# The last FFN's first batch: rows turned by VectorE's blocks and DMA instead of TensorE's transposes

## The chip, the cores and the metric

The kernel runs on one core of a Trainium2 chip. A core has five engines that run their own instruction streams and wait for one another by semaphores: TensorE (PE, matrix products; its weight loads are listed as PEld), VectorE (DVE), ScalarE (ACT), GpSimd (POOL) and SyncE (SP, which here only issues DMAs). The metric is the device time of one execution in microseconds, lower is better; a version's time is the median of its runs.

## The reference

Two transformer layers with post-layernorm, all float32, on `x` of 8 batches x 512 tokens x 512 features. The change lies where layer 1's attention meets layer 1's FFN:

```python
x = L0_attn_x
x = _layernorm(x + _L0_attn_ref(x, ...))    # 16 heads, causal
x = _layernorm(x + _L0_ffn_ref(x, ...))     # 8 experts, the two best per token, LoRA merged
x = _layernorm(x + _L1_attn_ref(x, ...))    # 8 query heads, 2 key/value heads of 64, no mask; adds its own input once more
x = _layernorm(x + _L1_ffn_ref(x, ...))

def _L1_ffn_ref(x, wq_gate, s_gate, wq_up, s_up, wq_down, s_down):
    def _qlinear(x, wq, scale):             # integer weights, hidden width 1408
        W = (wq.astype(jnp.float32) - 128.0) * scale[:, None]
        return jnp.einsum('bsd,hd->bsh', x, W)
    gate = jax.nn.silu(_qlinear(x, wq_gate, s_gate))
    up = _qlinear(x, wq_up, s_up)
    return _qlinear(gate * up, wq_down, s_down)
```

## The kernel before

A batch is 512 tokens: NT = 4 tiles of 128 tokens, and ND = 4 chunks of 128 features. `xs[b]` holds a batch with tokens on the partitions. A matrix product over the features needs them on the partitions, so each batch's rows must be turned before it enters a layer.

**Two ways to turn.** TensorE can transpose 128x128 blocks against an identity into PSUM. The class `Turn` does it without TensorE: `Turn.blocks` has VectorE transpose each token tile in blocks of 32x32 (line 88, one instruction for a tile, four for a batch); `Turn.out` writes the result to DRAM in four DMAs (line 93), and `Turn.back` reads it back in one (line 96), with the blocks at their places. The four writes wait for all four block transposes, the read waits for the four writes. The tokens of such a turned batch lie in another order within a chunk; `Turn.by_tile` gives a view of an array in that order, and whoever leaves the turned layout applies it once.

**Layer 1's attention** (`Attention1.batches`, line 1644). For each batch, 4 groups of query heads (`g`) times 4 key tiles (`kt`) make 16 units, handled in 8 *slots* of two units each. A slot does, in this order:

- `score` of its two units: on PE the scores, on ACT the exponential (line 1705) into `p`, a tile of four buffers, so that unit u takes the buffer of unit u - 4;
- `add` of the two units of the slot before: DVE sums the probabilities of a group into `total` (line 1713); the first key tile of a group is not added alone but together with the second;
- the slot's extra pieces, `todo[i]`;
- `product` of the two units of the slot before (PE, line 1724);
- where these closed a group, `normalise`: PE sums `total` over the keys (`rs`, line 1732), ACT reads the sums (line 995), DVE takes the reciprocal (line 1735) and multiplies (line 1742), GpSimd adds to a guard.

The extra pieces come from `plan(b)`: output projections of the batch before (`project`: PE line 1670, then DVE's residual line 1676 and statistics lines 1684 and 1685), the queries of groups 1 to 3 (`query`: PE line 1607, ACT's copy line 1609), and what prepares the next batch, among it that batch's rows turned by `Turn`. These read `hT`, the batch's turned rows: one buffer in the pool `c_own`. The last batch (`final`, b = 7) has no next batch to prepare. It has instead, in slots 0, 2, 4 and 6, the four pieces of `IntegerFfn.split` for the FFN's first batch, b = 0, whose rows have long been through their layernorm.

On PE, DVE, ACT and POOL the order of the instructions in this stage is the order of the program (`in_order`): an instruction that waits holds back all that stand behind it on its engine. SP's queue is placed by the framework. PSUM tiles named by `mm` rotate through two banks.

After the last slot the code adds and multiplies the last two units, projects token tile 0 over the first three groups, closes the last group with `normalise`, projects the rest, adds the residuals and takes the statistics; then the FFN begins.

**The last FFN** (`IntegerFfn`). Its products run in a faster format (F32R) on two halves of each value, so a batch's turned rows come as `high` (a cast) and `low` (the rest). For batch 0 `split` makes them: sixteen transposes on PE (line 1108, four for each chunk), ACT's cast out of PSUM (line 1109), DVE's subtraction (line 1110). For the later batches `blocks` and `parts` do it within the FFN: `Turn`, then the cast (line 1098) and the subtraction (line 1099) from SBUF. `hidden` makes the hidden layer (PE line 1143, ACT and DVE lines 1146 to 1154) and splits it again, for b > 0 through `by_tile` so that the tokens come back to their order:

```python
hT, *halves = [self.turns[0].by_tile(a, back) if b else a for a, back in ((hT, True), (high, False), (low, False))]
```

Of the kernel before, what the change touches and what calls it, by code (L numbers as in the profile page):

```python
# [9 lines left out]
F32 = mybir.dt.float32  # L10
# [4 lines left out]
ALU = mybir.AluOpType  # L15
# [3 lines left out]
P = 128  # L19
NB = 8  # L20
S = 512
D = 512
NT = S // P
ND = D // P
# [48 lines left out]
class Turn:  # L73
# [11 lines left out]
    def blocks(self, room, t, x):  # L85

        out = room.rearrange("p (j t c) -> p j t c", t=self.n, c=32)[:, :, t, :]
        self.nc.vector.transpose(out, x.rearrange("p (j c) -> p j c", c=32))
# [977 lines left out]
class IntegerFfn:  # L1066
# [13 lines left out]
        self.halves[b] = [pool.tile([P, ND, S], F32R, tag=f"rows{i}", name=f"x3_{part}")  # L1080
                          for i, part in enumerate(("high", "low"))]

    def blocks(self, b, t):

        if t == 0:
            self.room(b)
            self.turned = self.raw.tile([P, ND * S], F32, tag="turned", name="turned")
        turn = self.turns[b % 2]
        turn.blocks(self.turned, t, self.env.xs[b][:, t, :])
        if t == NT - 1:  # L1090
            turn.out(self.turned)
            turn.back(self.turned)

    def parts(self, b, c):
# [2 lines left out]
        x = self.turned[:, ts(c, S)]  # L1097
        self.nc.scalar.copy(high, x)
        self.nc.vector.tensor_tensor(low, x, high.bitcast(F32), ALU.subtract)

    def split(self, b, c, ps):

        nc = self.nc
        if c == 0:
            self.room(b)
        high, low = self.halves[b]
        for t in range(NT):
            nc.tensor.transpose(ps[:, ts(t, P)], self.env.xs[b][:, t, ts(c, P)], self.env.ident)
        nc.scalar.copy(high[:, c, :], ps)
        nc.vector.tensor_tensor(low[:, c, :], ps, high[:, c, :].bitcast(F32), ALU.subtract)  # L1110

    def run(self, held_out, last_norm):
        tc, nc, weights = self.env.tc, self.nc, self.weights
        with ExitStack() as phase:
            self.work = phase.enter_context(tc.tile_pool(name="d_work", bufs=1))
            self.p_gu = phase.enter_context(tc.tile_pool(name="d_gu", bufs=2, space=PSUM))
            self.p_o = phase.enter_context(tc.tile_pool(name="d_o", bufs=1, space=PSUM))
            weights.open(phase.enter_context(tc.tile_pool(name="d_weights", bufs=1)), 3 * NHID - weights.at)
            self.sd = self.work.tile([P, D], F32, name="sd")
            with tc.tile_pool(name="d_slots", bufs=1) as slots:  # L1120
                while weights.at < 3 * NHID:
                    weights.load(slots, 4, 3 * NHID)
                    weights.convert()
                nc.sync.dma_start(out=self.sd, in_=self.env.ins.s_down.partition_broadcast(P))
            with tc.tile_pool(name="d_raw", bufs=1) as self.raw:
                for b in range(NB - 1):
                    self.batch(b)
                    if b == 0:
                        last_norm()
                        ps = self.p_gu.tile([1, 1], F32, tag="g", name="ps_held")  # L1130
                        nc.scalar.dma_start(out=held_out, in_=self.guard.partitions_held(self.env.const, ps))
            self.late = phase.enter_context(tc.tile_pool(name="d_late", bufs=self.HELD))
            self.batch(NB - 1)

    def hidden(self, b, c, held):

        nc, vec, work, weights = self.nc, self.env.vec, self.work, self.weights
        g = self.p_gu.tile([P, S], F32, tag="g", name="ps_g1")
        u = self.p_gu.tile([P, S], F32, tag="u", name="ps_u1")
        for ps, w in ((g, weights(2 * c)), (u, weights(2 * c + 1))):  # L1140
            for dc in range(ND):
                for i, x in enumerate(self.halves[b]):
                    nc.tensor.matmul(ps, lhsT=w[:, ts(dc, P)], rhs=x[:, dc, :],  # L1143
                                     start=(dc, i) == (0, 0), stop=(dc, i) == (ND - 1, 1))
        sg = work.tile([P, S], F32, tag="sg", name="sg1", bufs=2)
        nc.scalar.activation(sg, g, AF.Silu, scale=vec[:, V_SG + c : V_SG + c + 1])
        hT = work.tile([P, S], F32, tag="hT", name="hT2", bufs=2)
        nc.vector.scalar_tensor_tensor(hT, u, vec[:, V_SU + c : V_SU + c + 1], sg, ALU.mult, ALU.mult)  # L1148
        high, low = (self.late.tile([P, S], F32R, tag=f"h{i}", name="h_late") if held else
                     work.tile([P, S], F32R, tag=f"h{i}", name="h_half", bufs=2) for i in range(2))  # L1150

        hT, *halves = [self.turns[0].by_tile(a, back) if b else a for a, back in ((hT, True), (high, False), (low, False))]
        nc.scalar.copy(halves[0], hT)
        nc.vector.tensor_tensor(halves[1], hT, halves[0].bitcast(F32), ALU.subtract)  # L1154
        return high, low
# [381 lines left out]
class Attention1:  # L1537
# [94 lines left out]
        for part in (self.w_qkv[:, c, :], self.w_qkv[:, ND : ND + 2, ts(c, P)]):  # L1632
            self.nc.scalar.mul(part, part, self.nss[:, c : c + 1])

    def run(self, weights, split):

        with ExitStack() as phase:
            self.work = work = phase.enter_context(self.env.tc.tile_pool(name="c_work", bufs=1, reuse_waits="tile"))
            p_sc = phase.enter_context(self.env.tc.tile_pool(name="c_sc", bufs=2, space=PSUM, reuse_waits="tile"))
            p_av = phase.enter_context(self.env.tc.tile_pool(name="c_av", bufs=2, space=PSUM, reuse_waits="tile"))  # L1640
            with in_order(self.env.tc, mybir.EngineType.DVE, mybir.EngineType.Activation, mybir.EngineType.Pool):
                return self.batches(work, p_sc, p_av, weights, split)

    def batches(self, work, p_sc, p_av, weights, split):
        env, nc, guard, state, HD = self.env, self.nc, self.guard, self.state, self.HD
        xs = env.xs
        scale = 1.0 / math.sqrt(HD)
# [97 lines left out]
        def plan(b):  # L1745


            todo = [[] for _ in range(ND * NT // 2)]
            here = pieces.pop(b)
            first, final = b == 0, b == NB - 1  # L1750
            if first:
                pieces[1] = self.prepare(1)
                todo[0] += [lambda t=t: pieces[1]["fetch"](t) for t in range(NT)]
            then = pieces.get(b + 1)
            if b:
                for t, i in enumerate((2, 3, 4, 7) if final else (2, 3, 4, 5)):
                    todo[i].append(lambda t=t: project(b - 1, t))
                if not final:
                    todo[6].append(lambda: norm(b - 1))
            for g, i in zip((1, 2, 3), (1, 3, 5) if first else (0, 1, 5) if final else (0, 1, 3)):  # L1760
                todo[i].append(lambda g=g: here["query"](g))
            if final:
                for c, i in enumerate((0, 2, 4, 6)):
                    todo[i].append(lambda c=c: split(0, c, self.mm([P, S], "ps_xT")))
            else:
                if first:

                    for t, i in ((2, 1), (3, 2)):
                        todo[i].append(lambda t=t: then["sum"](t))
                        todo[i + 2].append(lambda t=t: then["stat"](t))  # L1770
                for t, i in ((0, 1), (1, 2)) if first else ((0, 0), (1, 1), (2, 1), (3, 2)):
                    todo[i].append(lambda t=t: then["add"](t))
                if first:
                    todo[4].append(then["deviations"])

                    todo[5].insert(0, then["norm"])
                    todo[6] += [lambda c=c: then["turn"](c) for c in range(ND)]
                else:
                    todo[2].append(then["deviations"])
                    todo[3].append(then["norm"])  # L1780
                    todo[3] += [lambda t=t: then["blocks"](t) for t in range(NT)]
                todo[6].append(then["key"])
                todo[7] += [then["value"], lambda: then["query"](0)]
                if b + 2 < NB:
                    after = pieces[b + 2] = self.prepare(b + 2)
                    todo[7] += [lambda t=t: after["fetch"](t) for t in range(NT)]
            for i in (7,) if first else (1, 7) if final else (5, 7):
                todo[i] += [weights.convert, lambda: weights.load(work, 2, weights.FIRST)]
            return todo

        last = []
        for b in range(NB):
            for i, thunks in enumerate(plan(b)):
                units = [(b, u // NT, u % NT) for u in (2 * i, 2 * i + 1)]
                ps = [score(*unit) for unit in units]
# [29 lines left out]
def usual_pass(tc, ins, held_out):  # L1825
    nc = tc.nc
    with ExitStack() as ctx:
# [4 lines left out]
        with tc.tile_pool(name="a_mm", bufs=2, space=PSUM) as p_mm, ExitStack() as attn1_ctx:  # L1832
# [28 lines left out]
            weights = IntegerWeights(env, guard)  # L1861
            weights.open(ctx.enter_context(tc.tile_pool(name="c_weights", bufs=1, side="right")), weights.FIRST)
            ffn = IntegerFfn(env, guard, weights, rows, dram)
            last_norm = attention.run(weights, ffn.split)
        ffn.run(held_out, last_norm)


# [304 lines left out]
```

## Time and profile before

| | |
|---|---|
| median of 3 runs | 2221.11 us (2220.45 to 2225.37) |
| profiled execution | 2228.55 us, span 2226.8 us |
| mean granted TensorE clock | 0.993 |
| busy over the span | PE 98%, DVE 57%, ACT 28%, POOL 22% |
| sixteen transposes of `split` (line 1108), first and last start | 1648.1 and 1693.7 us |
| layer 1's last batch, from its first scores to the FFN's first product | 1643.1 to 1722.8 us |
| the FFN's batches 0, 1, 2 | 63.2, 63.0, 63.0 us |

A group's row in the profile names the line, the engine, the operation and its tiles (output <- inputs). Records of a timeline are merged: the first column is the start, the second the length of the whole run of instructions, `x4` their number, and the bracket the idle time of the engine before them and what ended it. TensorE's matrix products in float32 are recorded as two instructions each. The ends of PE's records are modelled and overlap their successors a little, so distances between starts are the better measure there. In a row of stretches stand the length, the busy time and number of instructions of PE, PEld, DVE, ACT and POOL, the granted clock, the DMA engines' share and GB/s.

### The profile page before, as it was taken

To read this page: it belongs to the slowest core of one execution; us is meant where nothing else is said; L and a number is where in the kernel's file an instruction comes from. 1 tells how busy PE (TensorE), PEld (TensorE's weight loads), DVE (VectorE), ACT (ScalarE), POOL (GpSimd) and SP (SyncE) were. 2 spreads that over 40 slices of the span, in tenths; PEclk is the share of its full clock that TensorE was granted. 3 is DMA by queue.
4 is the path that set the end of the run, shared out by engine and by line. 5 is a ranking of instruction groups with operands and counts; after the bars stand their busy time and mean duration, and the time that the engine had idled before them with its cause. 6 is when DMAs were issued, how large, how long until landed. Compare 5 with 4: busy or idle time off the path is not lost. (4 is left out here: it accounts for less than half of the span.)

```text
span 2226.8 us, 23678 instructions
## 1 busy us (share of the span) xinstructions
PE 2191.9 (98%) x9006; PEld 1116.6 (50%) x9006; DVE 1273.7 (57%) x2032; ACT 632.0 (28%) x917; POOL 487.6 (22%) x489
## 2 busy tenths in 40 slices
PE   9999999999999999999999999999999999999997
PEld 3344444444444444444443333333343778888876
DVE  3556666666666633323316887798757655555443
ACT  2332323323233232122124333223332222222222
POOL 2322423234132333122105222222211000000000
PEclk9999999999999899999999999999999999999999
DMA  8010101101022216888735212312110321111000
GB/s 297 20 57 1 57 10 48 58 1 58 5 71 94 85 57 181 227 218 214 191 114 193 80 57 86 95 55 77 45 32 13 109 78 57 57 57 57 20 20 21
DMA packets 146428, 182.20 MB, mean 82 GB/s; under 512 B 60530, under 2 KB 89202, under 8 KB 144514
## 3 DMA queue, kind: packets, MB, share of 16 engines
q1 hardware_dynamic: 135024, 144.91, 21.0%
q0 software_dynamic: 10560, 34.61, 5.5%
q8 instruction: 74, 1.21, 0.2%
q10 hardware_dynamic: 722, 1.07, 0.1%
q14 instruction: 48, 0.39, 0.1%
HBM read 117.38 MB, written 63.18 MB: 81 GB/s over the span
## 5 line engine op out<-in xcount | busy, mean ns | idle before, releaser
L903 PE MATMUL ps_gu<-experts,xrT 128*128 128x512 f32 (+1 forms) x520 | 248.8, 601 | 0.0
L1360 ACT ACTIVATE p<-sc 128x2048 f32<-128x2048 f32 (+1 forms) x96 | 152.8, 1592 | 190.0 <-PE sc L1356 183.1
L1148 DVE SCALAR_TENSOR_TENSOR hT<-ps_u,vec,sg 128x512 f32<-128x512 f32 x88 | 65.6, 745 | 195.2 <-PE ps_u L1143 195.2
L1365 POOL TENSOR_SCALAR_AFFINE_SELECT p<-p 128x512 f32<-128x512 f32 x128 | 91.6, 729 | 385.2 <-ACT p L1360 378.5
L1159 PE MATMUL ps_f<-ffn_w,h_half 128*128 128x512 f32 x672 | 170.2, 394 | 0.6 <-issue 0.4
L998 POOL TENSOR_TENSOR g_total<-g_total,r_inv 128x512 f32<-128x512 f32 x64 | 89.7, 1401 | 358.3 <-DVE r_inv L1735 283.0
L1705 ACT ACTIVATE p<-sc 128x1024 f32<-128x1024 f32 x128 | 124.0, 1021 | 105.9 <-PE sc L1702 100.8
L1735 DVE RECIPROCAL r_inv<-r_inv 128x512 f32<-128x512 f32 x32 | 107.1, 3346 | 78.8 <-ACT r_inv L995 78.8
L1388 DVE TENSOR_TENSOR p<-p 128x1536 f32<-128x1536 f32 (+2 forms) x96 | 129.4, 1348 | 39.2 <-POOL p L1365 22.2
L905 DVE TENSOR_TENSOR h<-ps_gu,h 128x256 f32<-128x256 f32 x67 | 28.4, 424 | 212.8 <-ACT h L904 212.8
L903 PEld LDWEIGHTS ps_gu<-experts,xrT 128*128 128x128 f32 x520 | 96.2, 197 | 89.7 <-issue 89.5
L1159 PEld LDWEIGHTS ps_f<-ffn_w,h_half 128*128 128x128 f32 x672 | 124.4, 188 | 33.0 <-DVE h_half L1154 5.6
L1143 PE MATMUL ps_g<-x_high,ffn_w 128*128 128x512 f32 x352 | 138.9, 395 | 0.8 <-DVE x L1676 0.8
L1143 PE MATMUL ps_g<-x_low,ffn_w 128*128 128x512 f32 x352 | 139.1, 395 | 0.0
L1143 PE MATMUL ps_u<-x_low,ffn_w 128*128 128x512 f32 x352 | 138.8, 394 | 0.0
L1143 PE MATMUL ps_u<-x_high,ffn_w 128*128 128x512 f32 x352 | 138.7, 394 | 0.0
L919 PE MATMUL ps_y<-experts,hT 128*128 128x512 f32 (+1 forms) x272 | 127.9, 593 | 0.5 <-ACT hT L913 0.5
L1702 PE MATMUL sc<-qT,kT 64*128 64x512 f32 x512 | 127.3, 615 | 1.0 <-ACT qT L1609 0.7
L1292 PE MATMUL ps_q<-experts 128*128 128x512 f32 x256 | 121.1, 615 | 4.4 <-DMA experts<-in_xT 4.4
L1724 PE MATMUL av<-p,v 128*64 128x512 f32 x512 | 123.8, 605 | 0.0
L1285 PE MATMUL ps_v<-experts 128*128 128x512 f32 x256 | 118.0, 609 | 3.3 <-DVE v L1287 3.3
L1670 PE MATMUL ps_o<-attn_out,aoT 128*128 128x512 f32 x256 | 117.9, 605 | 0.8 <-ACT r_inv L995 0.8
(262 smaller groups left out, 3438.5 us busy)
## 6 DMA issues: line engine op xcount, KB each, us to landing
results<-y SPq DMA_DIRECT2D x68, 256.0 KB, 2.3
turned<-turned SPq DMA_DIRECT2D x56, 256.0 KB, 4.1
pair<-xrT SPq DMA_DIRECT2D x25, 512.0 KB, 3.4
xrT<-pair SPq DMA_DIRECT2D x100, 128.0 KB, 4.5
x<-in_x SPq DMA_DIRECT2D x8, 1024.0 KB, 7.5
experts<-in_gate_up SPq DMA_DIRECT2D x8, 1024.0 KB, 10.8
rows<-x SPq DMA_DIRECT2D x32, 256.0 KB, 2.0
x<-rows SPq DMA_DIRECT2D x8, 1024.0 KB, 15.5
```

Of the source, the lines that this page charges most:

```text
L903: nc.tensor.matmul(ps, lhsT=xT[:, c, :], rhs=self.weights(i, c), start=c == 0, stop=c == ND - 1)
L919: self.nc.tensor.matmul(ps, lhsT=hT[:, c, :], rhs=self.weights(i, ND + c), start=c == 0, stop=c == self.NI - 1)
L1143: nc.tensor.matmul(ps, lhsT=w[:, ts(dc, P)], rhs=x[:, dc, :], start=(dc, i) == (0, 0), stop=(dc, i) == (ND - 1, 1))
L1159: self.nc.tensor.matmul(os[t], lhsT=h[:, ts(t, P)], rhs=self.weights(2 * NHID + c), start=(c, i) == (0, 0), stop=(c, i) == (NHID - 1, 1))
L1285: nc.tensor.matmul(ps, lhsT=xts[b][:, c, ts(t, P)], rhs=wv[:, c, :], start=c == 0, stop=c == ND - 1)
L1292: nc.tensor.matmul(ps, lhsT=wq[:, g, ts(c, P)], rhs=xts[b][:, c, :], start=c == 0, stop=c == ND - 1)
L1360: nc.scalar.activation(p, sc[:, :, :width], AF.Exp, scale=scale)
L1388: nc.vector.tensor_tensor(total[:, :, P * kt :], total[:, :, P * kt :], p[:, :, at : at + w], ALU.add)
L1670: nc.tensor.matmul(ps, lhsT=state[b]["aoT"][:, c, ts(t, P)], rhs=w_out[:, c, :], start=c == 0, stop=c == ND - 1)
L1702: nc.tensor.matmul(sc[:, j, :], lhsT=st["kT"][hs, ts(kt, P)], rhs=st["qT"][g][hs, :], start=True, stop=True)
L1705: nc.scalar.activation(p, sc, AF.Exp, scale=scale)
L1724: nc.tensor.matmul(st["av"][HD * j : HD * (j + 1), :], lhsT=st["v"][:, kt, HD * j : HD * (j + 1)], rhs=p[:, j, :], start=kt == 0, stop=kt ...
```

## The change

The last attention batch no longer calls `split`. It calls the FFN's own `blocks` and `parts` for batch 0, as the FFN does for its later batches:

- in slot 4, after the output projection that stands there, the four block transposes of batch 0's rows, into a new tile that takes the buffer of `hT`, followed by the four DMAs to DRAM and the one back;
- in slots 6, 6, 7 and 7, the cast and the subtraction of each chunk, from SBUF;
- so that `hT` is free in time, the last batch's query of group 3 goes from slot 5 to slot 3, where the middle batches have it;
- `hidden` applies `by_tile` to batch 0 too;
- `split` and its sixteen transposes are gone.

```diff
@@ class IntegerFfn
-    def blocks(self, b, t):
+    def blocks(self, b, t, room=None):
         if t == 0:
             self.room(b)
-            self.turned = self.raw.tile([P, ND * S], F32, tag="turned", name="turned")
+            self.turned = self.raw.tile([P, ND * S], F32, tag="turned", name="turned") if room is None else room
         turn = self.turns[b % 2]
         turn.blocks(self.turned, t, self.env.xs[b][:, t, :])
         if t == NT - 1:
...
-    def split(self, b, c, ps):
-
-        nc = self.nc
-        if c == 0:
-            self.room(b)
-        high, low = self.halves[b]
-        for t in range(NT):
-            nc.tensor.transpose(ps[:, ts(t, P)], self.env.xs[b][:, t, ts(c, P)], self.env.ident)
-        nc.scalar.copy(high[:, c, :], ps)
-        nc.vector.tensor_tensor(low[:, c, :], ps, high[:, c, :].bitcast(F32), ALU.subtract)
...
-        hT, *halves = [self.turns[0].by_tile(a, back) if b else a for a, back in ((hT, True), (high, False), (low, False))]
+        hT, *halves = [self.turns[0].by_tile(a, back) for a, back in ((hT, True), (high, False), (low, False))]
@@ class Attention1, plan(b); run and batches pass the FFN itself on in place of its split
-            for g, i in zip((1, 2, 3), (1, 3, 5) if first else (0, 1, 5) if final else (0, 1, 3)):
+            for g, i in zip((1, 2, 3), (1, 3, 5) if first else (0, 1, 3)):
                 todo[i].append(lambda g=g: here["query"](g))
             if final:
-                for c, i in enumerate((0, 2, 4, 6)):
-                    todo[i].append(lambda c=c: split(0, c, self.mm([P, S], "ps_xT")))
+
+                room = []
+                def blocks(t):
+                    if t == 0:
+                        room.append(self.own.tile([P, ND, S], F32, tag="hT", name="turned2"))
+                    ffn.blocks(0, t, room[0].rearrange("p k s -> p (k s)"))
+                todo[4] += [lambda t=t: blocks(t) for t in range(NT)]
+                for c, i in enumerate((6, 6, 7, 7)):
+                    todo[i].append(lambda c=c: ffn.parts(0, c))
```

More of the change, by code (lines that the diff above doesn't have):

```diff
@@ L1633, in scale, with run @@
             self.nc.scalar.mul(part, part, self.nss[:, c : c + 1])
-    def run(self, weights, split):
+    def run(self, weights, ffn):
         with ExitStack() as phase:
@@ L1641, in run, with batches @@
             with in_order(self.env.tc, mybir.EngineType.DVE, mybir.EngineType.Activation, mybir.EngineType.Pool):
-                return self.batches(work, p_sc, p_av, weights, split)
-    def batches(self, work, p_sc, p_av, weights, split):
+                return self.batches(work, p_sc, p_av, weights, ffn)
+    def batches(self, work, p_sc, p_av, weights, ffn):
         env, nc, guard, state, HD = self.env, self.nc, self.guard, self.state, self.HD
@@ L1863, in usual_pass @@
             ffn = IntegerFfn(env, guard, weights, rows, dram)
-            last_norm = attention.run(weights, ffn.split)
+            last_norm = attention.run(weights, ffn)
         ffn.run(held_out, last_norm)
```

## The prediction

> **What bounds the kernel now.** I read the page first, then the busy time by stretches, then the timeline of each engine over layer 1's last batch (a slot is two score units and the pieces listed for it), then the DMA issues, last the stretches in which TensorE's granted clock fell. The page's first line, and the stretch from slot 0's exponentials to the last FFN's first matmul:
>
> ```profile
> PE 2191.9 (98%) x9006; PEld 1116.6 (50%) x9006; DVE 1273.7 (57%) x2032; ACT 632.0 (28%) x917; POOL 487.6 (22%) x489
> 1644.31:1722.80 78.49, 76.81 (x257) 28.56 (x253) 51.46 (x52) 22.83 (x33) 9.50 (x7) 1.00 0.00 0
> ```
>
> TensorE is busy 76.8 of 78.5 us; VectorE follows with 51.5. A saving on PE counts only while DVE and ACT, whose order is the program's, keep up. PE's timeline, slots 0, 4, 5 and the end:
>
> ```profile
> 1648.54 0.60 PE L1108 MATMUL ps_xT<-ident,x 128*128 128x128 f32 x4
> 1649.06 1.94 PE L1724 MATMUL av<-p,v 128*64 128x512 f32 x8
> ...
> 1677.25 3.70 PE L1670 MATMUL ps_o<-attn_out,aoT 128*128 128x512 f32 x8
> ...
> 1685.96 3.70 PE L1607 MATMUL ps_q<-hT,attn_qkv 128*128 128x512 f32 x8
> ...
> 1708.59 1.08 PE L1732 MATMUL rs<-total,ones 128*64 128x512 f32 x4
> 1710.51 11.43 PE L1670 MATMUL ps_o<-attn_out,aoT 128*128 128x512 f32 x26 [0.84 <-ACT r_inv L995]
> 1722.78 0.50 PE L1143 MATMUL ps_g<-x_high,ffn_w 128*128 128x512 f32 x1 [0.84 <-DVE x L1676]
> ```
>
> Four transposes hold PE 0.52 us (1648.54 to 1649.06). The rs at 1708.59 (last group's softmax sums) needs VectorE's last two additions; behind it stand all 26 output records and the FFN. VectorE, and SyncE's queue for the same turn one batch earlier:
>
> ```profile
> 1608.86 2.48 DVE L88 STREAM_TRANSPOSE turned<-xn 128x512 f32<-128x512 f32 x4
> ...
> 1684.94 3.35 DVE L1735 RECIPROCAL r_inv<-r_inv 128x512 f32<-128x512 f32 x1 [1.68 <-ACT r_inv L995]
> 1688.40 0.69 DVE L1742 TENSOR_TENSOR aoT<-av,r_inv 128x512 f32<-128x512 f32 x1
> 1689.00 1.71 DVE L1713 TENSOR_TENSOR total<-p,p 128x1024 f32<-128x1024 f32 x1
> ...
> 1704.89 2.52 DVE L1713 TENSOR_TENSOR total<-total,p 128x1024 f32<-128x1024 f32 x2
> 1611.37 3.23 SPq L93 DMA_DIRECT2D turned<-turned  x4
> 1618.90 0.34 SPq L96 DMA_DIRECT2D hT<-turned  x1
> hT<-turned SPq DMA_DIRECT2D x7, 1024.0 KB, 4.8
> ```
>
> The additions end at 1707.41, 1.2 us before PE asks: that is VectorE's whole slack. A turn through DRAM costs, after the blocks, 6.5 to 7.7 us from the first write to the read back and 4.7 to 6.5 us until that lands.
>
> **Removed and moved.** The sixteen transposes: 0.52 + 0.53 + 0.53 + 0.58 = 2.2 us of PE in slots 0, 2, 4, 6. Query 3 (3.54 us of PE) goes from slot 5 to slot 3, as in the middle batches: PE's total is unchanged, slot 4 starts later, slot 5 shrinks to 3.8 us and slot 6 to 4.7. Casts and subtractions stay four and four (0.59 and 0.67 from PSUM before; 0.62 and 0.68 from SBUF in the FFN's rows), but leave slots 0, 2, 4, 6 for 6, 6, 7, 7.
>
> **Added.** Four block transposes on DVE (2.48 us) and five DMAs on SP. Nothing else stands on SP until the weight load at 1722.08, so their issue costs nothing. The room hT is free early: query 3 reads it last, in slot 3. In the FFN's first batch the split by tile changes form only: 0.62 against 0.62 us (cast), 0.68 against 0.69 (subtraction); 11 x 0.01 us beside PE, 0.1 if nothing hid it.
>
> **Where the time goes.** *Blocks:* slot 4's output projection ends at 1680.8 before; two transposes less (-1.05) and the query more (+3.54) make it 1683.3. Its residual and statistics, 1.6, stand ahead of the blocks: 1685.05; blocks done 1687.5. *Round trip:* 11 of the turns give 11.3 to 12.7 us from write to landing, one in heavier traffic 13.3; mean 12.0, so rows land at 1699.5.
>
> *ACT:* behind the blocks, DVE does slot 4's reciprocal (3.45), product (0.61) and unit 9's addition (1.64): 1693.25. That addition frees the probability buffers for slot 6's two exponentials (0.97 each), which so end at 1695.4. Next on ACT is the first cast, which waits for the DMA until 1699.5. Queued behind it: the second cast, the reading of group 2's sums, the exponentials of units 14 and 15, two more casts. DVE waits for those sums.
>
> *DVE from the landing:* two casts 1.06, reading the sums 0.72 (1701.3), reciprocal 3.45, product 0.61, unit 13's addition 1.64 (1707.0), residual and statistics of the fourth projection 1.6, two subtractions 1.22, additions of units 14 and 15 2.5: 1712.4. The last rs starts at 1712.5 instead of 1708.59: +3.9, the 2.2 saved already inside. From there the chain is unchanged and passes it on. With round trips of 11.3 to 12.7 it is +3.2 to +4.6, with 13.3 +5.2.
>
> *Clock:* PE now stands twice: about 2.3 us in slot 6 (rs of group 2 waits for DVE's additions, 1693.5 to 1695.8) and 3.8 us before the last rs. The trace of before shows what such a stop does:
>
> ```profile
> 278.97 5.40 PE L1285 MATMUL ps_v<-experts 128*128 128x512 f32 x8 [1.71 <-DVE v L1287]
> 280.00:281.00 1.00, 1.00 (x2) 0.34 (x1) 0.00 (x0) 0.00 (x0) 0.54 (x1) 0.50 0.00 0
> ```
>
> After 1.71 us idle the granted clock is 0.50 for 3.4 us, and eight records take 5.40 instead of 3.70: 1.7 lost. The stop of 1.77 us at 721.1 gave 0.50 for about 7 us, so up to 3.4; stops of 0.94 and less gave none. Slot 6's loss is hidden, as PE waits again later (3.8 shrinks to 2.1, still over 1.7). The loss after the last rs is on the path, as everything to the FFN is PE's. Bounds 0 and 3.4; I take 1.7, the nearest row. Sum: 3.9 + 1.7 = +5.6.
>
> [...]
>
> **Own time.** The profiled execution took 2228.55 us (span 2226.8), 7.4 over the median 2221.11. The change is a difference inside one stretch, so I add it to the median: 2226.7.
>
> **Rivals.** *No gain, no loss:* the rows are back before ACT asks, at a round trip of 7.9 us or less (1687.5 to 1695.4). Then DVE alone decides: sums of group 2 read by 1697.7, the same 3.45 + 0.61 + 1.64 + 1.6 + 1.22 + 2.5 make 1708.7, rs at 1708.8, +0.2: 2221.3. All twelve timed turns speak against it. *Faster:* the 2.2 us arrive in full, 2218.9: DVE would need its slack of 1.2 and 2.2 more while it gets 2.48 of blocks and two later subtractions; decided by whether its additions end before 1706.5. *The wait without the clock:* +3.9, 2225.0, if neither stop lowers the clock. *A worse stop:* round trip 12 to 13.3 and the clock low for 7 us: 3.9 to 5.2 plus 3.4, 2228.4 to 2229.7. *That the turn isn't done where it says:* the room could only be late if query 3 were, and that ends ten microseconds before the first block; I give it nothing.
>
> **How the numbers follow.** Forecast 0.55 (own range +4.9 to +6.9), wait without clock 0.15, worse stop 0.14, no change 0.10, faster 0.06. The three slower cases hold 0.84, from +3.2 to +8.6; allowing 0.8 below for the median's own spread (two of three runs lie within 0.7), the range is 2223.5 to 2229.8. About 0.2%, 4.4 us, is what a measurement of this kernel can tell from no change: forecast and worse stop are beyond it, the wait without clock is mostly not, nor are "no change" and the 2.2 us gain. So slower 0.71, same 0.26, faster 0.03 for what I haven't seen.
>
> **What would show it.** Right: in slot 6 ACT idle some 4 us before x_high, ended by the DMA turned<-turned; the last rs of layer 1 idle 2 to 4 us behind DVE total; the ps_o after it slowed at a granted clock near 0.5; no idle on PE before the first ps_g beyond its 0.84. Wrong: if the first cast follows the exponentials at once; if the last rs starts before 1709; if the turn lands under 8 us after the blocks; if PE loses its time in the FFN's batches rather than here.

## The result, and the profile after

The changed kernel is slower: 2230.02 us, median of 14 runs (2224.59 to 2233.72), beside 2223.43 us for the kernel before (14 runs, 2220.45 to 2226.49; the three known before the prediction are among them). The ratio is 1.0031, 95% interval 1.0022 to 1.0040, about +6.9 us. The profiled execution has a span of 2228.7 us.

The page's first line, and the stretch that answers to the one shown of before (from slot 0's exponentials to the last FFN's first product; columns as there):

```profile
PE 2186.2 (98%) x8990; PEld 1111.9 (50%) x8990; DVE 1272.7 (57%) x2036; ACT 632.6 (28%) x917; POOL 488.4 (22%) x489
1639.50:1724.20 84.70, 77.87 (x240) 27.52 (x236) 53.59 (x56) 22.65 (x33) 8.25 (x7) 0.96 0.09 25
```

The page still says 98%: it can't show this change. The stretch does: 84.7 us instead of 78.5, TensorE idle for 6.8 of them instead of 1.7, and a mean granted clock of 0.96. PE's timeline of the changed kernel, slots 5 to 7 and the end (line numbers are 11 lower than before):

```profile
1687.04 1.94 PE L1713 MATMUL av<-p,v 128*64 128x512 f32 x8
1691.21 1.08 PE L1721 MATMUL rs<-total,ones 128*64 128x512 f32 x4 [2.23 <-DVE total L1702]
...
1701.35 2.84 PE L1659 MATMUL ps_o<-attn_out,aoT 128*128 128x512 f32 x6
1707.17 1.64 PE L1721 MATMUL rs<-total,ones 128*64 128x512 f32 x4 [2.97 <-DVE total L1702]
1709.64 13.76 PE L1659 MATMUL ps_o<-attn_out,aoT 128*128 128x512 f32 x26 [0.83 <-ACT r_inv L995]
1724.24 0.50 PE L1132 MATMUL ps_g<-x_high,ffn_w 128*128 128x512 f32 x1 [0.84 <-DVE x L1665]
```

Both sums now wait for VectorE's additions, 2.23 and 2.97 us, and the 26 output records behind the last sums take 13.76 us where they took 11.43. The granted clock of that time is a stretch row's third number from the end:

```profile
1711.00:1713.00 2.00, 2.00 (x3) 0.67 (x2) 2.00 (x2) 0.00 (x0) 0.00 (x0) 0.50 0.00 0
1715.00:1717.00 2.00, 2.00 (x6) 0.95 (x5) 1.91 (x7) 0.00 (x0) 0.00 (x0) 1.00 0.00 0
```

The clock record has it at half from 1707.55 to 1714.38. Now the way there: VectorE's blocks, SyncE's DMAs, ScalarE, VectorE again:

```profile
1680.34 2.49 DVE L88 STREAM_TRANSPOSE turned<-x 128x512 f32<-128x512 f32 x4
...
1682.86 3.22 SPq L93 DMA_DIRECT2D turned<-turned  x4
1689.31 0.33 SPq L96 DMA_DIRECT2D turned<-turned  x1
...
1688.61 1.94 ACT L1694 ACTIVATE p<-sc 128x1024 f32<-128x1024 f32 x2 [4.16 <-DVE total L1702]
1694.29 1.14 ACT L1098 CAST x_high<-turned 128x512 fp32r<-128x512 f32 x2 [3.74 <-DMA turned<-turned]
1695.34 0.59 ACT L995 ACTIVATE r_inv<-rs 128x512 f32<-128x512 f32 x1
...
1696.16 3.35 DVE L1724 RECIPROCAL r_inv<-r_inv 128x512 f32<-128x512 f32 x1
...
1704.64 2.48 DVE L1702 TENSOR_TENSOR total<-total,p 128x1024 f32<-128x1024 f32 x2
```

ScalarE has slot 6's exponentials done at 1690.55 and then stands 3.74 us before the first cast, until the turned rows are back. The sums of group 2 lie ready since 1692.3 and are read only at 1695.34, behind the casts; VectorE's reciprocal follows, and its last additions end at 1707.12.

### The profile page after: what moved, and what is told of

It reads as the page before. It is cut to its first block, busy times and chain, and to the rows that moved or that the text cites. A ratio compares the mean times of both kernels' runs of the same rounds, so it can differ in the third digit from the quotient of the medians.

```text
span 2228.7 us, 23660 instructions
## 1 busy us (share of the span) xinstructions
PE 2186.2 (98%) x8990; PEld 1111.9 (50%) x8990; DVE 1272.7 (57%) x2036; ACT 632.6 (28%) x917; POOL 488.4 (22%) x489
## 5 line engine op out<-in xcount | busy, mean ns | idle before, releaser
L1289 PE MATMUL ps_k<-experts 128*128 128x512 f32 x256 | 117.5, 602 | 0.2 <-ACT r_inv L995 0.2
## 6 DMA issues: line engine op xcount, KB each, us to landing
x<-rows SPq DMA_DIRECT2D x8, 1024.0 KB, 11.3
```

The source lines that it names most:

```text
L1289: nc.tensor.matmul(ps, lhsT=wk[:, g, ts(c, P)], rhs=xts[b][:, c, :], start=c == 0, stop=c == ND - 1)
```

## The experiments

One kernel's runs lie some 6 to 9 us apart, and in the profiles the last batch begins anywhere from 1635.6 to 1643.1 us, so each run is also judged by a part of its profile: the *stretch* goes from the last batch's first scores to the FFN's first product, and *last sums* is the start of the last rs in it, counted from there. Each row's stretch is that of one execution. An interval of the ratio reaches 2 to 3 us to either side, so by time alone a step of 1 us can't be told from nothing.

| | last sums, us | stretch, us | against before | ratio to before (95% interval) |
|---|---|---|---|---|
| before | 65.5 | 79.7 | | 1 |
| changed | 68.9 | 86.0 | +6.3 | 1.0031 (1.0022 to 1.0040) |
| changed, again | 69.0 | 83.2 | +3.5 | 1.0037 (1.0023 to 1.0051) |
| query 3 moved alone | 66.7 | 80.9 | +1.2 | 1.0005 (0.9996 to 1.0014) |
| changed, no round trip | 67.5 | 81.7 | +2.0 | 1.0004 (0.9995 to 1.0013) |
| changed, stops overfilled | 71.2 | 86.2 | +6.5 | 1.0041 (1.0026 to 1.0055) |
| changed, stops filled | 69.0 | 83.2 | +3.5 | 1.0021 (1.0011 to 1.0031) |
| changed, blocks first | 65.4 | 79.6 | -0.1 | 0.9999 (0.9990 to 1.0008) |
| spread, with the turn by blocks | 63.6 | 77.8 | -1.9 | 0.9992 (0.9983 to 1.0001) |
| spread, with the transposes | 65.4 | 79.6 | -0.1 | 1.0002 (0.9993 to 1.0011) |

**The moved query alone**, in the kernel before:

```diff
-            for g, i in zip((1, 2, 3), (1, 3, 5) if first else (0, 1, 5) if final else (0, 1, 3)):
+            for g, i in zip((1, 2, 3), (1, 3, 5) if first else (0, 1, 3)):
```

> The kernel before with one part of the change: the last batch's query of group 3 in slot 3 instead of slot 5; the sixteen transposes stay. Stretch meant: from the last batch's first scores to the FFN's first product, 79.7 us before, 86.0 in the changed kernel. Theory A (the change costs time because ScalarE stands behind the first cast until the turned rows are back, and then because the clock halves after PE's stop): little here, as no DMA stands in the way. But slots 5 and 6 become short, and the sums of group 2 and the reciprocal of group 1 no longer fit: I work out a stop of 1.2 us on PE ahead of group 2's sums and +1.2 us in the stretch, no stop ahead of the last sums. Rival B (the moved query alone makes the slots too short for VectorE): +3 us or more, with stops at both sums. Rival C (the loss lies in the turned order of batch 0's rows or elsewhere in the program): 0.

Measured as theory A has it: one stop, and +1.2 us in the stretch.

```profile
1694.50 1.08 PE L1732 MATMUL rs<-total,ones 128*64 128x512 f32 x4 [1.18 <-DVE total L1713]
```

Slots 5 and 6 have too little on PE to cover VectorE's reciprocal, product and three additions. Rivals B and C fall: the query costs 1.2, neither most of the loss nor nothing.

**No round trip.** The first batch's casts read the rows as the block transposes left them:

```diff
-        if t == NT - 1:
+        if t == NT - 1 and b:
             turn.out(self.turned)
             turn.back(self.turned)
```

> The changed kernel without the five DMAs of batch 0's turn: the casts read the rows as the block transposes left them, so batch 0's rows enter the FFN in the wrong places. VectorE's four block transposes, the late casts and subtractions and the moved query are all kept. Theory A: ScalarE casts right behind slot 6's exponentials; the last sums start 0.3 us later than before, counted from the batch's first scores (after: 3.4 later); PE still stops some 2.2 us ahead of group 2's sums; stretch 80.0 us if the clock holds, 83 if that stop halves it. Rival D (VectorE's added work is the delay, the transfer is hidden behind it): the last sums as late as in the changed kernel, stretch 86.

ScalarE casts at once, and the last sums lose their stop. The stop in slot 6 stays at 2.23 us, and here it is the one after which the clock halves (0.50 from 1693 to 1695):

```profile
1691.76 1.14 ACT L1098 CAST x_high<-turned 128x512 fp32r<-128x512 f32 x2
...
1692.53 1.97 PE L1721 MATMUL rs<-total,ones 128*64 128x512 f32 x4 [2.23 <-DVE total L1702]
1694.43 2.71 PE L1691 MATMUL sc<-qT,kT 64*128 64x512 f32 x8
...
1707.06 1.08 PE L1721 MATMUL rs<-total,ones 128*64 128x512 f32 x4
```

The stretch lies between the two values given, 2.0 over before: rs and scores took 4.55 us to the next product (1692.53 to 1697.08) where the changed kernel has 2.93 (1691.21 to 1694.14), so 1.6 of the 2.0 is the clock and 0.4 is the rest (0.3 worked out). Rival D falls: without the wait VectorE's added work costs next to nothing net. It does eat the 2.1 us that the transposes gave back.

**Blocks first.** The same instructions, the four block transposes ahead of slot 4's projection:

```diff
-                todo[4] += [lambda t=t: blocks(t) for t in range(NT)]
+                todo[4] = [lambda t=t: blocks(t) for t in range(NT)] + todo[4]
```

> The changed kernel with the four block transposes ahead of slot 4's output projection in program order, not behind it: nothing else moves. They then don't wait for that projection's residual and end about 4.5 us sooner after slot 4's start, so the turned rows should land 4 us sooner, near the end of slot 6's exponentials. Theory A: ScalarE's wait for the DMA falls from 3.74 us to under 1, the last sums start within 0.5 us of where they do before (worked out: -0.3), PE stops about 1.7 us ahead of group 2's sums; stretch 79.4 to 80 us, up to 3 more if that stop halves the clock. Rival D (VectorE's amount of work decides, not the landing): same work, so 85 to 86.

```profile
1672.56 2.48 DVE L88 STREAM_TRANSPOSE turned<-x 128x512 f32<-128x512 f32 x4
...
1687.84 1.94 ACT L1694 ACTIVATE p<-sc 128x1024 f32<-128x1024 f32 x2 [3.68 <-DVE total L1702]
1689.66 1.14 ACT L1098 CAST x_high<-turned 128x512 fp32r<-128x512 f32 x2
...
1690.43 1.08 PE L1721 MATMUL rs<-total,ones 128*64 128x512 f32 x4 [1.75 <-DVE total L1702]
...
1703.35 1.08 PE L1721 MATMUL rs<-total,ones 128*64 128x512 f32 x4
```

No wait ahead of the cast, a stop of 1.75 us in slot 6 with the clock at 1.00, none ahead of the last sums, and the stretch is that of before. Where four instructions stand in VectorE's order decides between +6.9 us and nothing: behind the projection they wait for PE's 3.6 us and a residual that they don't need.

**Stops filled.** To separate the clock from the wait, PE gets products to do while it stops; their result is overwritten:

```diff
             rs = self.mm([P, S], "rs1")
+            for _ in range({2: 4, 3: 6}.get(g, 0) if b == NB - 1 else 0):
+                nc.tensor.matmul(rs[:HD, :], lhsT=ones, rhs=w_out[:, 0, :], start=True, stop=True)
```

> The changed kernel with idle products added on PE where it stops: 4 ahead of group 2's sums and 6 ahead of the last ones, into the bank that the sums then overwrite (1.9 and 2.9 us, within the stops of 2.23 and 2.97). Nothing that PE, ACT or DVE wait for changes. Theory A with the clock as its second half: the granted clock stays at 1.00, the 26 output records take about 11.5 us as before and not 13.8, the stretch is 83.1 us: 2.9 less than in the changed kernel, 3.4 over the one before. Rival E (PE is slower after the last sums for another reason, such as its operands or VectorE's traffic): still 13.8, stretch 86.

I had sized the products at 0.48 us each; they took about 0.86 (two records each, 0.43 us from start to start), overran the stops, and the last sums came 2.3 us later. What the run does show is the clock: 1.00 throughout, and the output records back to 11.43 us. The stretch, 86.2, equals rival E's number, but for the overrun and not for slow records. So again, with 2 and 3 products (the 0.79 us in the expectation misreads the same records; at 0.86 they still fit into the stops):

> The changed kernel with fewer idle products than in the run before, which overran the stops: 2 ahead of group 2's sums and 3 ahead of the last ones, at 0.79 us each by that run (1.6 of 2.23 us and 2.4 of 2.97). Theory A: the last sums start as in the changed kernel, 68.9 us after the batch's first scores; the granted clock stays at 1.00 and the stretch is 83.1 us, 3.4 over the kernel before, in the time 3 to 4 us over it, with less spread than the changed kernel. Rival E: 86.0.

```profile
1686.18 1.88 PE L1721 MATMUL rs<-attn_out,ones 128*64 128x512 f32 x4
1688.59 1.08 PE L1723 MATMUL rs<-total,ones 128*64 128x512 f32 x4 [0.52 <-DVE total L1702]
...
1704.61 1.08 PE L1723 MATMUL rs<-total,ones 128*64 128x512 f32 x4 [0.32 <-DVE total L1702]
1706.53 11.43 PE L1659 MATMUL ps_o<-attn_out,aoT 128*128 128x512 f32 x26 [0.84 <-ACT r_inv L995]
```

The last sums are as late as in the changed kernel (69.0), the records behind them take 11.43, the clock is 1.00, the stretch 83.2: rival E falls. The time, +4.6 us by the ratio, is within its interval of the 3.5 of the stretch; its spread of 7.1 us is no smaller than the 6.7 of the run beside it, against what I expected. Its nine runs have a mean granted clock of 0.994 to 0.997, on average 0.995, like the kernel before; the five runs of the changed kernel beside it have 0.993 each. So the lower clock is usual in the changed kernel and not a chance of one profile.

**The changed kernel once more**, beside it:

> The changed kernel once more, as the measure for the three beside it. Theory A (the wait for the turned rows, +3.4 us in the stretch from the last batch's first scores to the FFN's first product, then a clock that halves after PE's stops, by chance of their place): the last sums again 68.9 us after the batch's first scores; the stretch between 83.1 us (no halving) and 86.0; time 3 to 9 us over the kernel before. Rival E (PE slower after the last sums for another reason): 86.0 each time.

```profile
1690.76 1.95 PE L1721 MATMUL rs<-total,ones 128*64 128x512 f32 x4 [2.23 <-DVE total L1702]
1692.64 2.76 PE L1691 MATMUL sc<-qT,kT 64*128 64x512 f32 x8
...
1706.84 1.08 PE L1721 MATMUL rs<-total,ones 128*64 128x512 f32 x4 [1.46 <-DVE total L1702]
1708.76 11.43 PE L1659 MATMUL ps_o<-attn_out,aoT 128*128 128x512 f32 x26 [0.84 <-ACT r_inv L995]
```

In this execution the clock halved after slot 6's stop instead (0.50 from 1691 to 1694). That loss is hidden in the wait behind it, since PE would have waited later anyway (the second stop is 1.46 instead of 2.97), and 1.46 did not halve it again: stretch 83.2. The same program, halved at another stop, differs by 2.8 us.

**Spread.** The cure that the runs point to: blocks right behind query 3 in slot 3, and a projection in slot 6:

```diff
-                for t, i in enumerate((2, 3, 4, 7) if final else (2, 3, 4, 5)):
+                for t, i in enumerate((2, 4, 6, 7) if final else (2, 3, 4, 5)):
...
-                todo[4] += [lambda t=t: blocks(t) for t in range(NT)]
-                for c, i in enumerate((6, 6, 7, 7)):
+                todo[3] += [lambda t=t: blocks(t) for t in range(NT)]
+                for c, i in enumerate((6, 6, 6, 7)):
```

> The changed kernel with its pieces spread otherwise: output projections in slots 2, 4, 6, 7 instead of 2, 3, 4, 7, so that slot 6 is no longer short; the four block transposes at the end of slot 3, right behind query 3; casts and subtractions in slots 6, 6, 6, 7. Theory A: the rows land before ScalarE asks and VectorE's additions are done before PE's sums, so the sixteen transposes' 2.1 us come through: last sums 63.4 us after the batch's first scores, stretch 77.6 us, no stop over 1 us, clock 1.00; time 2.1 us (0.1%) under the kernel before, about what five rounds can just tell. Rival D (VectorE's added work uses the saving up wherever it stands): stretch 79.7 or more.

```profile
1688.63 1.03 PE L1721 MATMUL rs<-total,ones 128*64 128x512 f32 x4
...
1701.50 1.08 PE L1721 MATMUL rs<-total,ones 128*64 128x512 f32 x4
1703.41 11.43 PE L1659 MATMUL ps_o<-attn_out,aoT 128*128 128x512 f32 x26 [0.84 <-ACT r_inv L995]
```

No stop ahead of the sums of either group, and the stretch is 77.8: the transposes' time comes through, 1.9 us. Its control, the same spreading around the sixteen transposes:

> The kernel before, its sixteen transposes kept in slots 0, 2, 4, 6, with only the spreading of the run beside it: query 3 in slot 3, output projections in slots 2, 4, 6, 7. It separates what the spreading is worth from what the turn by blocks is worth. Theory A: nothing, as PE's work is the same and no stop arises: stretch 79.7 us, time within 1 us of the kernel before; the 2.1 us of the run beside it are then the transposes'. Rival F (the gain is the spreading's): stretch 77.6.

79.6: the spreading by itself gives nothing, so the 1.8 between the two is what the turn by blocks is worth. In the time it is at the edge of what can be told, so it ran again:

> The spread version once more for its time, which the first five rounds left at a ratio of 0.9992, interval 0.9983 to 1.0001. Theory A: the stretch again 77.8 us, 1.9 under the kernel before, so a ratio near 0.9991, and both sets together clear of 1. Rival D: a ratio at or above 1.0000.

Again 77.8 in the stretch, and 0.9992 (0.9983 to 1.0002; 2222.85 us beside 2225.27). Each interval just reaches 1; put together by their widths (an estimate), they would end just under it, as expected. The two sets agree, and the profile places the gain where it was expected; by time alone it is at the edge of what can be told.

## Why the prediction was right or wrong

The direction and the mechanism were right: slower, because ScalarE stands behind the first cast and the last sums come late. What failed is the base that the difference was added to, and next to it the size of the clock's term. Step by step:

- *Removed:* 2.2 us of PE. The spread version, with no stop left, gives 1.9.
- *Round trip:* 12.0 us taken, 11.5 measured (blocks done at 1682.83, cast at 1694.29), inside the rows' 11.3 to 12.7. ScalarE's wait was 3.74 us for 4.1 worked out.
- *Last sums:* +3.9 forecast, +3.4 measured; the 0.5 is about the shorter round trip. Stops of 2.3 and 3.8 us forecast, 2.23 and 2.97 found; the query's share in the first, 1.2 by itself, was inside the sum but not named as a cost of its own.
- *The clock is the mis-sized term of the sum.* Forecast +1.7 on the path, with bounds 0 and 3.4. The profiled execution lost 2.9 (17.07 us from the last sums to the FFN instead of 14.19), as the clock stayed at half for 6.8 us; another execution lost none on the path. I had taken both stops to halve it each time; in the profiles one or the other did. My reading that stops of 0.94 us and less gave none did not cover every fall either: in the trace of before the clock also fell at 740.33 and 794.94, where PE had been busy for 3.39 and 3.41 of the 3.41 us ahead.
- *Sum and base:* +5.6 forecast, +6.3 in the profiled stretch, +6.9 by the ratio of the runs. The median, 2230.02, lies 0.2 above the range's end all the same. The step that failed is "so I add it to the median: 2226.7": the median of three runs was 2221.11, while the kernel before had 2223.43 over 14. Of the 3.3 us by which the measured median lies above 2226.7, 2.3 are this base and 1.0 the change itself. I allowed 0.8 for the base's spread, and only downwards. Two values within 0.7 of each other said little, with the third 4.3 away; and the profiled execution, 2228.55, which I set aside, was a fourth value on the high side: with it the median would have been 2223.24.
- *Rivals:* "no gain, no loss" is what the kernel does without the round trip and before the clock (0.4 over before), or with the blocks first (0.1 under); its condition, the rows back when ScalarE asks, was the right one. "The wait without the clock" is, in its stretch, the second profile of the changed kernel, though the clock did fall there.

In sum, of the stretch's +6.3: transposes -2.1; query moved +1.2; the blocks and late casts on VectorE about +1.2 (what is left of the 0.3 worked out for no round trip); the wait for the rows about +3.1; the clock +2.9. VectorE's part and the wait are differences of runs and workings, not measured by themselves.

The rest of the program holds little of the loss: from the FFN's first product to the end of the span the profiles have 504.0 us before, 504.5 in both of the changed kernel, and 504.1 to 504.5 in the others.

Left open: how much of the runs' +6.9 is the clock's. The runs with the stops filled put the part without it at 2.4 to 6.9 us by their interval, which doesn't settle it. Nor is it shown what decides which stop halves the clock in a given execution; the last section has the stops and the clock behind each.

## What to carry to other kernels

Where engines run in program order, put a DMA-bound step as early in the order as its data allow, and its reader late: what counted here was not the transfer but what was queued behind the instruction that waits for it (a stretch of 86.0 us with the block transposes behind the projection, 79.6 with the same ones ahead of it). Before moving work off the bound engine, check slot by slot that the others still finish in time; a piece moved out of a slot takes its cover away from them (1.2 us for the query). And a stop of the bound engine can cost more than its length (2.9 us more behind the one of 2.97 us), so price the clock with it, and give a forecast as a difference unless the base is known well.

## What the runs showed of the hardware

**Where the granted clock changed.** In the trace of before, the changes of TensorE's granted clock lie whole numbers of 3.413 us apart (the falls at 279.53 and 805.18 us: 154 times that), and in the changed kernel's trace too (734.75 and 1707.55 us: 285 times). A *step* is such a stretch of 3.413 us here. Counted back to the span's start, the first border lies at 3.05 us before and at 0.89 us in the changed kernel. For the other runs the borders are laid through their own changes of clock, as windows of 1 and 4 us show them. How much of a stop fell into one step, and the clock behind it:

| trace and stop | stop, us | PE idle in each step that it touches, us | granted clock behind it |
|---|---|---|---|
| changed, slot 6 | 2.23 | 1.50 and 0.73 | 1.00 |
| changed, last sums | 2.97 | 2.97 | 0.50 for two steps |
| changed again, slot 6 | 2.23 | 2.23 | 0.50 for one step |
| changed again, last sums | 1.46 | 1.46 | 1.00 |
| no round trip, slot 6 | 2.23 | 2.22 and 0.01 | 0.50 for one step |
| blocks first, slot 6 | 1.75 | 1.75 | 1.00 |
| query moved alone, between 276 and 280 | 2.09 in all | not shown | 1.00 |
| before, ahead of 278.97 | 1.71 | 1.71 | 0.50 for one step |
| before, at 721.1 | 1.77 | 1.77 | 0.50 for two steps |

In the changed kernel the stop of 2.23 us, cut in two by a border, cost no more than its length; with no round trip the same length lay in one step but for 0.01 us and cost 1.6 us on top. The rows give no single threshold: behind 1.71 us the clock was 0.50, behind 1.75 it was 1.00. What makes it fall, and why it stays low for one step or for two, is not shown.

**Products side by side.** The products added as a filler were dearer than the 0.48 us that I had put them at: 128x512 against 64 columns, always into the same 64 partitions of the tile, took 0.86 us each back to back (stops overfilled). The two of the sums, one into each half of the partitions, take 0.96 together in the changed kernel (1645.57 to 1646.53): their records start in pairs 0.007 us apart there, while the filler's start one by one, 0.43 us apart.
